# Adding pairs of exponential tiles by accumulating DMAs in the softmax sums of a fused attention and mixture-of-experts block

## The chip, the cores and the metric

The kernel runs on one core of one Trainium2 chip, in one launch. The metric is the device time of a run in microseconds. Of the kernel before there are three runs, and one more that was profiled.

## The reference, cut to what matters

The reference is a transformer block with layer norms behind both halves: attention with LoRA on its four projections, then a mixture of eight experts plus a shared expert. The change lies in the attention, and there in the sums of the softmax.

```python
q, k, v = (split(lora_linear(x, ...)) for each)      # x: 2 x 1024 x 512, 16 heads of 32
scores = jnp.einsum('bhqd,bhkd->bhqk', q, k) * HEAD_DIM ** -0.5
attn = jax.nn.softmax(scores, axis=-1)               # divides by the sum over the 1024 keys
out = jnp.einsum('bhqk,bhkd->bhqd', attn, v)
x = layernorm(x + lora_linear(out, Wo, ...))
x = layernorm(x + moe(x))
```

## The kernel before

The program has three parts: projections with the folding of LoRA, attention, and the output projection's end with the experts. In the profile the attention runs from 158 to 624 us of the span.

The attention is cut into **16 units**, u = 0 to 15. A unit is one group of four heads and 512 queries of one batch. It has **eight steps**, kc = 0 to 7, one for each block of 128 keys; step t is 8u + kc, and "k3" means the step in which kc is 3. The order inside a step is written out by hand and holds on every engine (`manual_schedule` over all five), so an instruction waits for all that stand before it on its own engine. In a step stand:

- four scores matmuls (`st`, L569, one for each head), each followed on ScalarE by the exponential (L578). Two heads share one tile of 128x1024, so a step fills two tiles `pts[t, 0]` and `pts[t, 1]`, called pair 0 and pair 1 here. The tiles lie in `PTB = 13` buffers of one pool.
- four matmuls of another kind (`s`, L182), which compute the scores of the unit to come with queries in the rows, twelve steps ahead (`LEAD`). VectorE takes a maximum out of each (L190). They go through three PSUM banks: a fourth `s` matmul waits until the first has been read. The maxima of a unit are transposed in k4 (`finish_max`, L200) and shift the exponentials of a later unit.
- between the second and the third scores matmul, `av_step` of the step before: eight matmuls (L599) that multiply the exponentials of step t - 1 with the values.

The sums over the keys are formed by whole-tile additions. `add_step(t, pr)` (L588) makes the tile of kc = 0 the accumulator `accs[u, pr]` at no cost and adds the tiles of kc = 1 to 6 to it; kc = 7 is not added but goes into the sum matmuls directly (`DIRECT`). An addition is on VectorE where `ON_DVE` says so, for (1, 0) and (2, 1), and otherwise on GpSimd: ten on GpSimd and two on VectorE in each of the units 0 to 13. The addition (1, 0) is issued early, within k1 (`EARLY`); the others are issued in `av_step`, one step after their tile's. The last two units have a table of their own (`DVE_END`).

In k3 of the next unit, `finish` (L622) multiplies the two accumulators and the two tiles of kc = 7 with ones: 16 matmuls behind that step's `av` matmuls. ScalarE copies the sums out, small DMAs on the SP queue carry them through DRAM to a reciprocal on VectorE (`invert`, issued at the end of k4) and back, and in k7 the outputs are scaled (`normalize`).

GpSimd has other work in the same queue: it adds the output bias to a residual tile (`add_res`, L674) in k1 of each unit from 1 on, and in k5 of the units 12 and 13 as well. During the units 8 and 9 the output projection of the first batch is woven in (L691), which makes these two units about 10 us longer.

Of the kernel before, what the change touches and what calls it, by code (L numbers as in the profile page):

```python
# [2 lines left out]

# [10 lines left out]
ALU = mybir.AluOpType  # L14
# [39 lines left out]
FIN = 3  # L54
REC = 4
XTB = 5
ON_DVE = ((1, 0), (2, 1))
EARLY = (1, 0)
OPROJ_AT = (65, 67, 69, 71, 73, 75, 77, 79)
RES_AT = tuple(8 * i + 6 for i in range(8)) + (70, 78, 86, 94, 98, 102, 106, 110)  # L60
# [9 lines left out]
DVE_END = {  # L70
    NU - 2: ((1, 0), (2, 1), (4, 1), (5, 1), (6, 0), (6, 1), (7, 0), (7, 1)),
    NU - 1: ((1, 0), (2, 0), (3, 0), (4, 0), (5, 0), (6, 0), (6, 1)),
}
# [19 lines left out]
def kernel(  # L93
# [3 lines left out]
    pe, act, dve, pool, sp = nc.tensor, nc.scalar, nc.vector, nc.gpsimd, nc.sync  # L97
# [74 lines left out]
    mts, pts, avs, accs, vts = {}, {}, {}, {}, {}  # L172
# [377 lines left out]
    with ph2, tc.manual_schedule(engines={mybir.EngineType.PE}):  # L550
# [31 lines left out]
        def add_step(t, pr):  # L582
            u, kc = t // 8, t % 8
            if kc == 0:
                accs[u, pr] = pts[t, pr]
            elif kc not in direct(u):
                eng = dve if (kc, pr) in DVE_END.get(u, ON_DVE) else pool
                eng.tensor_tensor(accs[u, pr], accs[u, pr], pts[t, pr], ALU.add)  # L588

        def early(t, pr):  # L590
            return t // 8 not in DVE_END and (t % 8, pr) == EARLY

        def av_step(t):
            u, kc = t // 8, t % 8
            g = u // 2
            if kc == 0:
                avs[u] = avp.tile([P, 512], F32, name=f"av{u}", tag="av")
            for h in range(4):
                pe.matmul(  # L599
                    avs[u][32 * h : 32 * h + 32, :],  # L600
                    vts[g][:, kc, 32 * h : 32 * h + 32],
                    pts[t, h // 2][:, h % 2, :],
                    start=kc == 0,
                    stop=kc == 7,
                    skip_group_check=True,
                )
            for pr in range(2):
                if not early(t, pr):
                    add_step(t, pr)

        def direct(u):
            return () if u in NO_DIR else DIRECT
# [98 lines left out]
        for t in range(NS):  # L711
            u, k = t // 8, t % 8
# [17 lines left out]
            if t:  # L730
                between[1].append(lambda: av_step(t - 1))
                if u and k == (FINE if u == NU - 1 else FIN):
                    between[1].append(lambda: finish(u - 1))
# [19 lines left out]
            if t - NS >= OPROJ1:  # L753
                next(op10, None)
        av_step(NS - 1)
        finish(NU - 1)
        normalize(NU - 1, (0,))
# [302 lines left out]
    for st in range(NB):  # L1060
# [18 lines left out]
        if st == NB - 3:  # L1079
            reads_xd(  # L1080
                sp.dma_start(
                    out=meta, in_=xd_d[:, D : D + 2].rearrange("(j p) c -> p j c", p=P)
# [7 lines left out]
    with tc.manual_schedule(engines=MAN4):  # L1090
        last = None
        for e in range(E):
            nxt = e + 1
            hss = []
            for c in range(6):
# [32 lines left out]
                if e:  # L1128
                    for hf in range(2):
                        j = 2 * (e - 1) + hf  # L1130
# [7 lines left out]
        for hf in range(2):  # L1138
            j = 2 * (E - 1) + hf
# [65 lines left out]
```

## Time and profile before

| what | value |
|---|---|
| median of three runs | 1076.01 us (1075.66 to 1076.06) |
| time of the profiled execution | 1076.59 us |
| its span in the profile | 1074.9 us, so 1.69 us lie around the span |
| granted TensorE clock | 0.993 |
| busy share of the span, PE / VectorE / ScalarE / GpSimd | 97 / 70 / 49 / 53 % |
| attention, 158.15 to 624.36 us: busy PE / VectorE / ScalarE / GpSimd | 451.0 / 416.6 / 290.4 / 385.1 us of 466.2 |

The span is the time from the first to the last instruction of one profiled execution. Busy time is a union of the intervals in which an engine works, so a share near one says that an engine is hardly ever without an instruction, and not that it is at its peak.

### The profile page before, as it was taken

How to read it: one execution, taken by the hardware profiler on the slowest of the kernel's cores; microseconds unless marked ns; L12 is line 12 of the kernel's file. 1: busy time of each engine (PE TensorE's matmuls, PEld its weight loads, DVE VectorE, ACT ScalarE, POOL GpSimd, SP SyncE). 2: the span in 40 equal slices, each digit the busy share in tenths (PEclk: the TensorE clock that was granted, in tenths of full speed). 3: DMA queues.
4: the chain of work that ended last, by engine and by line, in shares of the span. 5: the costliest groups of instructions: out<-in, count | busy, mean ns of one | idle time of the engine just before them, and what ended most of it. 6: DMA issues, size and time to landing. Idle time of an engine off the chain costs nothing. (4 is left out here: it accounts for less than half of the span.)

```text
span 1074.9 us, 16446 instructions
## 1 busy us (share of the span) xinstructions
PE 1038.9 (97%) x5992; PEld 742.9 (69%) x5992; DVE 748.3 (70%) x1217; ACT 530.1 (49%) x1026; POOL 573.1 (53%) x379
## 2 busy tenths in 40 slices
PE   8999999999999999999999999999999999999996
PEld 6888774444444455544444369889999998888885
DVE  6732788999999987799998784233522556777762
ACT  5422215666666655556666756222222455555552
POOL 5000007888888877868899575000050045666674
PEclk8999999999999999999999999999999999999999
DMA  8866860141414242042520123000082556777731
GB/s 279 288 219 202 252 195 25 52 110 48 103 47 106 71 109 70 22 90 70 119 81 22 51 60 109 20 21 20 31 240 95 161 184 207 234 234 235 237 107 59
DMA packets 77585, 131.24 MB, mean 122 GB/s; under 512 B 14344, under 2 KB 23048, under 8 KB 77504
## 3 DMA queue, kind: packets, MB, share of 16 engines
q1 hardware_dynamic: 73664, 117.59, 37.6%
q0 software_dynamic: 3840, 12.60, 3.3%
q8 instruction: 47, 0.77, 0.3%
q14 instruction: 34, 0.28, 0.1%
HBM read 96.10 MB, written 33.80 MB: 121 GB/s over the span
## 5 line engine op out<-in xcount | busy, mean ns | idle before, releaser
L588 POOL TENSOR_TENSOR pt<-pt,pt 128x1024 f32<-128x1024 f32 x151 | 360.5, 2413 | 207.7 <-ACT pt L578 190.6
L190 DVE TENSOR_REDUCE mt<-s 128x1 f32<-128x512 f32 x512 | 323.4, 680 | 39.7 <-PE s L182 39.6
L578 ACT ACTIVATE pt<-st 128x512 f32<-128x512 f32 x512 | 270.8, 602 | 141.4 <-PE st L569 137.6
L569 PE MATMUL st<-qs,ks 98*128 98x512 f32 x512 | 215.6, 432 | 1.9 <-ACT pt L578 1.2
L182 PE MATMUL s<-ks,qs 96*128 96x512 f32 x512 | 203.0, 404 | 12.7 <-DVE mt L190 11.5
L569 PEld LDWEIGHTS st<-qs,ks 98*128 98x128 f32 x512 | 96.0, 189 | 136.4 <-issue 87.2
L817 POOL TENSOR_TENSOR w2s<-w2r,w2s 128x512 fp32r<-128x512 f32 x42 | 65.7, 1582 | 127.0 <-ACT w2s L816 103.1
L829 PE MATMUL h<-xthe,w13s 128*128 128x256 f32 x704 | 131.4, 284 | 1.5 <-DVE hs L850 1.5
L182 PEld LDWEIGHTS s<-ks,qs 96*128 96x128 f32 x512 | 97.2, 190 | 41.3 <-DVE mt L190 26.8
L829 PEld LDWEIGHTS h<-xthe,w13s 128*128 128x128 f32 x704 | 111.0, 191 | 3.0 <-DVE hs L850 2.7
L829 PE MATMUL h<-xtle,w13s 128*128 128x256 f32 x352 | 100.2, 285 | 0.0
L588 DVE TENSOR_TENSOR pt<-pt,pt 128x1024 f32<-128x1024 f32 x43 | 91.4, 2131 | 3.3 <-ACT pt L578 2.9
L599 PE MATMUL av<-pt,vt 128*32 128x512 f32 x512 | 75.0, 605 | 0.0
L599 PE MATMUL av<-pt,x1b 128*32 128x512 f32 x512 | 68.8, 609 | 0.0
L829 PEld LDWEIGHTS h<-xtle,w13s 128*128 128x128 f32 x352 | 67.3, 191 | 0.7
L977 POOL DMA_INDIRECT xd_d<-x1a,slot_i x8 | 8.0, 996 | 111.8 <-DVE slot_i L974 109.7
L873 PE MATMUL y<-w2s,hs 128*128 128x512 f32 x260 | 62.7, 394 | 2.9 <-POOL w2s L817 2.9
L873 PEld LDWEIGHTS y<-w2s,hs 128*128 128x128 f32 x260 | 47.4, 188 | 15.7 <-POOL w2s L817 6.7
L297 PE MATMUL o<-xh,wh 128*128 128x512 f32 x128 | 51.1, 399 | 3.0 <-ACT wh L271 3.0
L312 ACT ACTIVATE oh<-o,bqk_sb 128x512 fp32r<-128x512 f32 x32 | 22.0, 690 | 59.0 <-PE o L297 56.5
L297 PE MATMUL o<-xl,wh 128*128 128x512 f32 x128 | 50.9, 398 | 0.0
L297 PE MATMUL o<-xh,wl 128*128 128x512 f32 x128 | 50.9, 397 | 0.0
(819 smaller groups left out, 1758.5 us busy)
## 6 DMA issues: line engine op xcount, KB each, us to landing
qs<-qkd SPq DMA_DIRECT2D x48, 256.0 KB, 5.6
ks<-qkd SPq DMA_DIRECT2D x24, 512.0 KB, 6.8
x1a<-in_w_dram SPq DMA_DIRECT2D x24, 512.0 KB, 6.8
w2r<-in_w_dram SPq DMA_DIRECT2D x42, 256.0 KB, 3.2
qkd<-oh SPq DMA_DIRECT2D x32, 256.0 KB, 2.7
qkd<-ol SPq DMA_DIRECT2D x32, 256.0 KB, 2.6
x1b<-in_w_dram SPq DMA_DIRECT2D x16, 512.0 KB, 5.7
x1b<-in_wT_dram SPq DMA_DIRECT2D x16, 256.0 KB, 5.3
```

What stands on the lines that cost most here:

```text
L182: pe.matmul(s1, Qs[u % 3][0:96, h, qt * P : qt * P + P], Ks[g % 2][0:96, h, kh * 512 : kh * 512 + 512], start=True, stop=True,)
L190: dve.tensor_reduce(mts[u][:, c, kh : kh + 1], s1, AX.X, ALU.max)
L297: pe.matmul(o, lhs, rhs, start=k + i == 0, stop=k + i == KC + 1)
L312: act.activation(oh, o, AF.Identity, bias=bias)
L569: pe.matmul(sb, Ks[g % 2][:, h, kc * P : kc * P + P], Qs[u % 3][:, h, :], start=True, stop=True,)
L578: act.activation(pts[t, h // 2][:, h % 2, :], sb, AF.Exp, scale=SCALE)
L588: eng.tensor_tensor(accs[u, pr], accs[u, pr], pts[t, pr], ALU.add)
L599: pe.matmul(avs[u][32 * h : 32 * h + 32, :], vts[g][:, kc, 32 * h : 32 * h + 32], pts[t, h // 2][:, h % 2, :], start=kc == 0, stop=kc == 7 ...
L817: pool.tensor_tensor(hl[:, 1, :], raw, f(hl[:, 0, :]), ALU.subtract)
L829: pe.matmul(hp[:, j * 256 : j * 256 + 256], lhs, rhs[:, k, :], start=n == 0, stop=n == 11,)
L873: pe.matmul(o, lhs, rhs, start=n == 0, stop=n == 16)
L977: sc_ = pool.indirect_dma_start(out=xd_d, out_offset=bass.IndirectOffsetOnAxis(ap=slot_i[:, i : i + 1], axis=0), in_=x1[i // 8][:, i % 8, ...
```

## The change

In the units 0 to 13 the tiles of kc = 2 are no longer added to the accumulators by an engine. In their place GpSimd's queue issues, in `av_step` of kc = 3, one DMA for each pair that adds the tile of kc = 2 to the tile of kc = 3 in SBUF (`accum_op=ALU.add`, 512 KB each). The sum of both, standing in the tile of kc = 3, is added to the accumulator on GpSimd one step later, behind the additions of kc = 4. VectorE keeps the addition (1, 0) alone. The units 14 and 15 are as before.

```diff
-ON_DVE = ((1, 0), (2, 1))
+ON_DVE = ((1, 0),)
+DMA_LATE = 1
...
-            for pr in range(2):
-                if not early(t, pr):
-                    add_step(t, pr)
+
+            for d, pr in product((0, DMA_LATE), range(2)):
+                j = kc - d
+                if u in DVE_END:
+                    if d == 0:
+                        add_step(t, pr)
+                elif j == 3 and d == 0:
+                    pool.dma_start(out=pts[t, pr], in_=pts[t - 1, pr], accum_op=ALU.add)
+                elif (j == 3) == (d > 0) and j >= 0 and j != 2 and not early(t - d, pr):
+                    add_step(t - d, pr)
```

The order of a unit's work on GpSimd becomes: the addition (1, 1); the two DMAs; the additions (4, 0), (4, 1), (3, 0), (3, 1), (5, 0), (5, 1), (6, 0), (6, 1). In the built program GpSimd goes from 377 to 391 instructions and VectorE from 1212 to 1198.

## The prediction

> **What bounds the kernel now.** I read the page's busy rows and groups first, then the timelines of VectorE, PE and GpSimd in unit 5 (299.35 to 327.19 us), then the DMA rows. The page:
>
> ```profile
> L588 POOL TENSOR_TENSOR pt<-pt,pt 128x1024 f32<-128x1024 f32 x151 | 360.5, 2413 | 207.7 <-ACT pt L578 190.6
> L190 DVE TENSOR_REDUCE mt<-s 128x1 f32<-128x512 f32 x512 | 323.4, 680 | 39.7 <-PE s L182 39.6
> L182 PE MATMUL s<-ks,qs 96*128 96x512 f32 x512 | 203.0, 404 | 12.7 <-DVE mt L190 11.5
> ...
> L588 DVE TENSOR_TENSOR pt<-pt,pt 128x1024 f32<-128x1024 f32 x43 | 91.4, 2131 | 3.3 <-ACT pt L578 2.9
> ...
> L977 POOL DMA_INDIRECT xd_d<-x1a,slot_i x8 | 8.0, 996 | 111.8 <-DVE slot_i L974 109.7
> ```
>
> PE is the engine that is never without work. It loses only 11.5 us to VectorE by this row, but delays that hide inside stretched matmuls add to that, so I take step lengths. In PE's timeline the scores matmuls that open the steps of unit 5 stand at 299.35, 302.42, 305.49, 308.95, 313.73, 317.71, 321.05, 324.13 and 327.19: steps k0 to k7 of 3.07, 3.07, 3.46, 4.78, 3.98, 3.34, 3.08 and 3.06 us, in all 27.84. An undisturbed step is 3.07; k3 has the sums in addition. What can be won is in k2 (0.4 over) and k4 (0.9 over). PE, timeline, unit 5:
>
> ```profile
> 306.49 0.49 PE L182 MATMUL s<-ks,qs 96*128 96x512 f32 x1
> ...
> 310.86 1.90 PE L622 MATMUL sm<-pt,ones 128*32 128x512 f32 x16
> ...
> 315.09 0.50 PE L182 MATMUL s<-ks,qs 96*128 96x512 f32 x1 [0.50 <-DVE mt L190]
> 315.53 1.07 PE L599 MATMUL av<-pt,x1b 128*32 128x512 f32 x8
> ```
>
> VectorE and GpSimd over the same stretch (start, duration, count at the end, idle time before in brackets):
>
> ```profile
> 304.61 1.23 DVE L588 TENSOR_TENSOR pt<-pt,pt 128x1024 f32<-128x1024 f32 x1
> 305.75 2.48 DVE L190 TENSOR_REDUCE mt<-s 128x1 f32<-128x512 f32 x4
> ...
> 311.08 3.35 DVE L588 TENSOR_TENSOR pt<-pt,pt 128x1024 f32<-128x1024 f32 x1
> 314.36 1.28 DVE L190 TENSOR_REDUCE mt<-s 128x1 f32<-128x512 f32 x2
> ```
>
> ```profile
> 303.19 1.28 POOL L674 TENSOR_TENSOR x1a<-x1a,bo_bc 128x512 f32<-128x512 f32 x1
> 306.20 7.16 POOL L588 TENSOR_TENSOR pt<-pt,pt 128x1024 f32<-128x1024 f32 x3 [1.73 <-ACT pt L578]
> 314.58 14.09 POOL L588 TENSOR_TENSOR pt<-pt,pt 128x1024 f32<-128x1024 f32 x6 [1.23 <-DVE pt L588]
> ```
>
> The reader is to see this: the same VectorE addition takes **1.23 us** at 304.61, while GpSimd is idle (304.47 to 306.20), and **3.35** at 311.08, where a GpSimd addition is under way until 313.36 (306.20 + 7.16). 3.35 is 2.28 of waiting and 1.07 of adding. The long one keeps VectorE from the maxima, so the `s` matmul due at 314.43 starts at 315.09.
>
> **What the Trainium skill says.** "SBUF — State Buffer", section "Who interferes with whom": a VectorE instruction with two SBUF inputs contends with a GpSimd instruction that reads SBUF, and the second one to issue blocks until the first is done; `tensor_reduce` never contends on trn2. The trace agrees: 1.23 against 3.35, and maxima every 0.62 us beside a busy GpSimd. "DMA: Bandwidth & Descriptors", section "SWDGE vs HWDGE vs iDMA": a DMA that accumulates is issued from GpSimd, whose cores write its descriptors. The trace of before has only indirect ones (0.96 to 1.05 us of GpSimd each, mostly). "Collectives: The Full Stack", section "The bandwidth ceiling: the fold count and why AG ≠ RS ≠ AR": an adding transfer reads two sources for each write, and ran at half of a copy's rate. No row of before shows an accumulating DMA.
>
> **The change part by part.** Clock zero is the start of k4.
>
> *VectorE's addition (2, 1) goes* (14 of them). Without it `s` starts at 314.43, `av` 0.32 later at 314.75 and not at 315.53: **0.77 us** of k4 in each of the units 1 to 7, 10, 11 and 12, 7.7 in all. Unit 13 has a k4 of 3.70, worth 0.5. In unit 0 no sums cover the addition and PE shows 2.18 us idle at 174.54: 2.4. In units 8 and 9 the projection's matmuls lie between, idle 0.53 and 0.56: 0.6 each. Sum **-11.8**.
>
> *GpSimd's chain moves.* One addition per unit goes (10 to 9, 14 in all, 2.35 us each back to back), but the unit's eight late additions now stand behind two DMAs that wait for the `av` matmuls of kc = 3, which PE ends 2.09 after k4 starts. Before, the additions began in k2, at 306.20, as tiles came. Issue: 0.15 idle ahead of a DMA in the trace, 0.97 each, 0.305 between two, 0.03 to the next addition: the first addition starts at 2.09 + 0.15 + 0.97 + 0.305 + 0.97 + 0.03 = **4.5**. Additions then end at 6.9, 9.2, 11.6, 13.9, 16.3, **18.6**, 21.0 and 23.3.
>
> *What this meets.* VectorE's remaining addition comes 2.19 after k1 starts (304.61 - 302.42), which is 3.21 + 3.34 + 3.08 + 3.06 + 3.07 + 2.19 = **17.95**. Before, GpSimd was idle then. Now its sixth addition runs until 18.6, so VectorE is blocked for 0.65 first. Its 1.23 cost k2 0.4 (three PSUM banks absorb the rest), and all beyond costs PE in full: **+0.65** in k1 or k2 of the units 1 to 8, 11 and 12, 6.5 in all. Units 9 and 10 follow the long units, where GpSimd is done by then: 0. Unit 13 follows a unit with a bias addition in k5 (1.25): 1.9 against 0.75 lost there now, +1.15. In unit 14 the sums of 13 come about 1.2 late for the same 1.25. Sum **+8.85**.
>
> *The sums.* With VectorE's addition between them the last two GpSimd additions end at 24.4; `sm` is due at 22.93 + 1.91 = 24.84. Slack 0.45, hidden, and gone with half a microsecond more.
>
> *The transfers.* They share 16 DMA engines with SP's: nothing large is in flight (loads come in k0 and k6), but the small ones that carry the reciprocal are (`r` lands 3.05 after k4 starts, `rb` at 9.9 for a use at 12). The first must land by 9.2, 7.0 after its issue; the second by 11.6, 8.1 after. Loads of 512 KB land in 3.9 to 6.8 us, 256 KB in 2.7 to 5.6. Twice the reading makes 512 KB like 1 MB: from the quiet values 2.7 and 3.9, about 6.3, an estimate. So it is in time, and costs nothing; if the 6.8 were doubled, 13.6, GpSimd would be 6.6 late in each unit.
>
> *Buffers.* In the built program the exponential tiles of the next unit reuse freed tiles; the closest is (5, 0), 3 us after GpSimd's (1, 1) addition ends. No SP instruction moves; ScalarE has the same work.
>
> *Sum:* -11.8 + 8.85 = **-3.0 us** on the profiled 1076.59, which is 0.58 above the median: 1076.01 - 3.0 = **1073.0**.
>
> *Bounds of the unknown issue time* i (nearest row 0.97). Lateness is 2(i - 0.97) and weighs on ten units. At 0.7 the block is 0.11: -8.4. Under 0.64 the sixth addition is over and VectorE meets the whole seventh, 2.35: +14. At 1.12 the gain is gone. At 1.9 (two descriptors read per written one, twice the row) the lateness is 1.86: about +16.
>
> **The rivals.** *(a) The remaining addition is blocked longer (slower).* Place: VectorE in k1, against a GpSimd chain that is later, or earlier, by a fraction of 2.35 us. For it: 18.6 and 17.95 are 0.65 apart, and reading both operands may make the issue dearer than an indirect one. Against: the nearest row is steady. It decides from an issue of 1.12 us; at 1.5 the loss is 10 x 1.06 - 3.0 = +7.6, **1083.6**. *(b) The transfers land late (slower too).* GpSimd waits in front of (3, 0), `sm` waits for GpSimd, and every microsecond late costs one in 11 units: 1 us late makes -3 + 11 = +8, **1084**; 2 us, 1095. For it: a margin near 1 us over my estimate. Against: loads of the same size land within 6.8. *(c) The GpSimd chain falls just behind VectorE's addition,* issue about 0.7: **1067.6**. *(d) No difference:* what k4 gains k1 loses, **1076**, at issues near 1.1.
>
> **How the numbers follow.** The forecast with (c) as its good end, 1065 to 1073.8: 0.5. (d): 0.12. (a): 0.2. (b): 0.18. A measurement of this kernel tells 0.2%, 2.15 us, from no change. Faster 0.5, same 0.12, slower 0.38. The range is 1065 to 1091: down to no block at all with a little more, up to (a) at 1.9 or (b) at 1.6 us late. The forecast's own range is 1065 to 1074.
>
> **What would show it.** Right: k4 near 3.2 us, no VectorE L588 in k3, DMA issues near 1 us, a VectorE addition in k1 of about 1.9 us, k2 near 4.1, `sm` not waiting. Wrong: a VectorE addition of 3 us in k1 with k2 over 4.9 (a); GpSimd idle in front of L589 with a DMA as the releaser, and k3 over 5 (b); a k4 that stays at 3.9, which would mean that (2, 1) was not what delayed it.

## The result, and the profile after

The changed kernel takes **1180.59 us**, the median of four runs (1179.74 to 1183.92), against 1076.03 for the kernel before, run beside it: a ratio of **1.0978**, with a 95% interval from 1.0955 to 1.1001. The profiled execution took 1179.74 us with a span of 1178.0 and a granted TensorE clock of 0.946, where before it was 0.993.

First the groups of the page that answer to those of before. Behind the bar stand busy time, the mean of one in ns, and the idle time in front with what ended most of it.

```profile
L589 POOL TENSOR_TENSOR pt<-pt,pt 128x1024 f32<-128x1024 f32 x137 | 340.7, 2881 | 167.5 <-PE s L183 147.7
L191 DVE TENSOR_REDUCE mt<-s 128x1 f32<-128x512 f32 x512 | 324.4, 680 | 105.2 <-PE s L183 104.9
...
L183 PE MATMUL s<-ks,qs 96*128 96x512 f32 x512 | 215.4, 428 | 72.8 <-DVE mt L191 72.7
...
L615 POOL DMA_DIRECT2D pt<-pt x28 | 25.1, 1041 | 149.0 <-PE st L570 142.8
L589 DVE TENSOR_TENSOR pt<-pt,pt 128x1024 f32<-128x1024 f32 x29 | 91.4, 3161 | 6.0 <-PE av L600 2.8
```

The reader is to see three things. VectorE makes 29 additions instead of 43 and spends the same 91.4 us on them, so one takes 3.16 us instead of 2.13. The maxima `mt` and the `s` matmuls now wait for each other: 105 us on VectorE's side, 73 on PE's, where PE lost 11.5 before. And an addition on GpSimd reads 2.88 us, although additions in a row still begin 2.33 apart.

The step lengths say where. Unit 5 began at 299.35 before and begins at 334.02 now; in us:

| | k0 | k1 | k2 | k3 | k4 | k5 | k6 | k7 | unit |
|---|---|---|---|---|---|---|---|---|---|
| before | 3.07 | 3.06 | 3.46 | 4.78 | 3.97 | 3.34 | 3.08 | 3.06 | 27.83 |
| after | **6.79** | 3.08 | **10.28** | 4.80 | 3.21 | 3.34 | 3.07 | 3.07 | 37.64 |

k4 lost 0.76 us, as the change was to do. k0 grew by 3.7 and k2 by 6.8. PE's timeline of this unit (start, duration, idle time before and what ended it):

```profile
336.04 0.49 PE L183 MATMUL s<-ks,qs 96*128 96x512 f32 x1 [1.62 <-DVE mt L191]
...
341.84 1.07 PE L600 MATMUL av<-pt,x1b 128*32 128x512 f32 x8
...
349.70 0.79 PE L183 MATMUL s<-ks,qs 96*128 96x512 f32 x1 [4.96 <-DVE mt L191]
350.43 1.94 PE L600 MATMUL av<-pt,x1b 128*32 128x512 f32 x8
```

Both stalls end with a maximum of VectorE's. What VectorE did meanwhile:

```profile
334.70 0.70 DVE L669 TENSOR_TENSOR av<-av,rb 128x512 f32<-128x512 f32 x1 [2.13 <-DMA rb<-rd]
...
343.04 6.01 DVE L589 TENSOR_TENSOR pt<-pt,pt 128x1024 f32<-128x1024 f32 x1
348.97 2.47 DVE L191 TENSOR_REDUCE mt<-s 128x1 f32<-128x512 f32 x4
```

GpSimd over the same stretch:

```profile
323.99 1.77 POOL L615 DMA_DIRECT2D pt<-pt  x2 [13.73 <-PE st L570]
325.14 19.30 POOL L589 TENSOR_TENSOR pt<-pt,pt 128x1024 f32<-128x1024 f32 x8
343.82 1.85 POOL L682 TENSOR_TENSOR x1a<-x1a,bo_bc 128x512 f32<-128x512 f32 x1
345.06 2.90 POOL L589 TENSOR_TENSOR pt<-pt,pt 128x1024 f32<-128x1024 f32 x1
```

**The stall in k2** is the addition (1, 0) at 343.04. The eighth addition of GpSimd's row ends at 325.14 + 19.30 = 344.44, the residual's at 345.67, (1, 1) at 347.96, and VectorE's addition ends 1.09 later. It was held out not for the addition under way but until GpSimd's whole row was over. It depends on none of these three by its data.

**The stall in k0** is `normalize`, which waits for `rb`. The list of transfers has the median time from issue to landing at the end of a row; after:

```profile
pt<-pt POOLq DMA_DIRECT2D x28, 512.0 KB, 6.0
...
rd<-r SPq DMA_DIRECT2D x14, 8.0 KB, 5.1
```

before:

```profile
rd<-r SPq DMA_DIRECT2D x14, 8.0 KB, 1.6
```

The 8 KB of `rd` land 5.1 us after their issue instead of 1.6. In unit 1, counted from the start of k4, the two accumulating transfers are issued at 2.64 and 3.22 and land at 7.15 and 9.71; `rd` is issued at 4.89, and the first `rb` follows at 9.94, 0.2 us after the second transfer is in. `rb` lands at 12.8, and VectorE's scaling, which stands in k7 and was due at 12 before, slips into k0.

**A third part** no instruction waits for. After a stall PE's matmuls are slow: the `av` block at 350.43 takes 1.94 us, that at 341.84 took 1.07. Windows of unit 5 (the clock is the column behind the five engines):

```profile
337.13:340.54 3.41, 3.41 (x12) 1.37 (x12) 1.98 (x5) 1.36 (x3) 3.41 (x3) 0.50 0.48 115
...
343.89:349.60 5.71, 0.86 (x4) 0.38 (x2) 5.71 (x3) 1.61 (x4) 4.06 (x3) 0.80 0.00 0
349.60:354.17 4.57, 4.47 (x14) 1.98 (x14) 2.46 (x5) 0.79 (x2) 0.00 (x0) 0.50 0.00 0
354.17:358.97 4.80, 4.80 (x33) 2.14 (x32) 2.23 (x5) 2.39 (x5) 0.00 (x0) 1.00 0.00 0
```

Behind the idle 5 us the granted clock is 0.50 until k3 begins. Of the 7.2 us that k2 has over an undisturbed 3.07, about 5.1 are the gap in front of the `s` matmul and 2.1 are slow matmuls. The Trainium skill, "TensorE: Matmul & The Clock Gate", section "Part 1: The HAM clock gate (the "warmup" mystery)", says that after an idle window of some 3.4 us the clock is gated to 4/8 and comes back after a busy window. The two values are those of this trace, 0.50 and 1.00. The idle time is not: in k0 PE stood still for only 1.62 us, until 336.04, and the clock was 0.50 from 337.13 to 340.54 all the same.

### The profile page after: what moved, and what is told of

Its sections match the earlier page's. It is cut to its first block, busy times and chain, and to the rows that moved or that the text cites. A ratio compares the mean times of both kernels' runs of the same rounds, so it can differ in the third digit from the quotient of the medians.

```text
span 1178.0 us, 16463 instructions
## 1 busy us (share of the span) xinstructions
PE 1080.2 (92%) x5992; PEld 757.1 (64%) x5992; DVE 753.0 (64%) x1203; ACT 533.1 (45%) x1026; POOL 562.9 (48%) x393
## 4 chain that ended last, share of the span: by engine, by line
PE 62%; DVE 14%; DMA 10%; issue 5%; POOL 4%; ACT 2%; SPq 1%; POOLq 0%; DVEq 0%; ACTq 0%
PE av L600 9%; PE st L570 8%; PE o L298 7%; PE s L183 7%; DVE pt L589 5%; DMA rd<-r 5%; DVE mt L191 4%; PE op L699 3%; PE v L324 3%; PE h L837 3%; POOL w2s L825 3%; PE sm L630 2%; DMA rb<-rd 2%; DVE w13s L518 2%; SPq L658 1%
## 5 line engine op out<-in xcount | busy, mean ns | idle before, releaser
L589 POOL TENSOR_TENSOR pt<-pt,pt 128x1024 f32<-128x1024 f32 x137 | 340.7, 2881 | 167.5 <-PE s L183 147.7
L579 ACT ACTIVATE pt<-st 128x512 f32<-128x512 f32 x512 | 274.2, 602 | 209.4 <-PE st L570 203.1
L183 PE MATMUL s<-ks,qs 96*128 96x512 f32 x512 | 215.4, 428 | 72.8 <-DVE mt L191 72.7
L570 PE MATMUL st<-qs,ks 98*128 98x512 f32 x512 | 228.6, 457 | 2.1 <-ACT pt L579 1.2
L570 PEld LDWEIGHTS st<-qs,ks 98*128 98x128 f32 x512 | 102.9, 203 | 157.5 <-issue 103.6
L183 PEld LDWEIGHTS s<-ks,qs 96*128 96x128 f32 x512 | 105.4, 206 | 101.9 <-DVE mt L191 86.3
L615 POOL DMA_DIRECT2D pt<-pt x28 | 25.1, 1041 | 149.0 <-PE st L570 142.8
L589 DVE TENSOR_TENSOR pt<-pt,pt 128x1024 f32<-128x1024 f32 x29 | 91.4, 3161 | 6.0 <-PE av L600 2.8
L600 PE MATMUL av<-pt,vt 128*32 128x512 f32 x512 | 81.6, 661 | 0.0
L600 PE MATMUL av<-pt,x1b 128*32 128x512 f32 x512 | 80.3, 704 | 0.0
L881 PEld LDWEIGHTS y<-w2s,hs 128*128 128x128 f32 x260 | 47.4, 188 | 15.8 <-POOL w2s L825 6.7
```

The source lines that it names most:

```text
L183: pe.matmul(s1, Qs[u % 3][0:96, h, qt * P : qt * P + P], Ks[g % 2][0:96, h, kh * 512 : kh * 512 + 512], start=True, stop=True,)
L570: pe.matmul(sb, Ks[g % 2][:, h, kc * P : kc * P + P], Qs[u % 3][:, h, :], start=True, stop=True,)
L579: act.activation(pts[t, h // 2][:, h % 2, :], sb, AF.Exp, scale=SCALE)
L600: pe.matmul(avs[u][32 * h : 32 * h + 32, :], vts[g][:, kc, 32 * h : 32 * h + 32], pts[t, h // 2][:, h % 2, :], start=kc == 0, stop=kc == 7 ...
L881: pe.matmul(o, lhs, rhs, start=n == 0, stop=n == 16)
```

## The experiments

A single run is compared with the kernel before on the same chip, where that took 1087.9 us (E1 to E4), 1075.5 (E5 to E8), 1087.7 (E14 to E16) or the median named.

### E1 and E2: the transfers left out, or turned into plain copies

```diff
-   pool.dma_start(out=pts[t, pr], in_=pts[t - 1, pr], accum_op=ALU.add)
+   pass                                                          # E1
+   pool.dma_start(out=pts[t, pr], in_=pts[t - 1, pr])            # E2
```

> The changed kernel without its 28 accumulating DMAs; the tiles of kc = 2 are left out of the sums of units 0 to 13, and 1.0 is added to each sum in the copy on ScalarE so that none is zero. Two theories on the 6.6 us that k2 grew by: (train) VectorE's addition in k1 waits until GpSimd's whole unbroken row of additions is over, not just the one under way; (DMA) the DMAs bring it about. Train: the row now starts when the exponentials of k4 are there, and holds its nine tile additions and the bias addition without a gap until about 24 us after k4 starts; VectorE's addition comes at 18, takes 4 to 7 us, k2 is 6 to 9.5 us. DMA: k2 is back at 3.5. On the 3.7 us that k0 grew by: (queue) the reciprocal's store waits behind the accumulating DMAs; then k0 is back at 3.1. (late chain) GpSimd's later additions delay it; then k0 stays near 6.8. Train with queue: 1076 - 12 + 11 x 5 = about 1120 (1095 to 1140); DMA with queue: 1065 to 1072.

> The changed kernel with its 28 DMAs as plain copies of the same tiles from the same queue: the tile of kc = 2 replaces that of kc = 3 in place of being added (kc = 3 is left out of the sums), and 1.0 is added to each sum. Queue theory, by volume: the reciprocal's store still lands with the second copy; copies read half, so the second lands about 5.0 us after k4 starts plus 3, near 8.2 and not 9.7, and k0 grows by 1.5 to 2.5 us instead of 3.7. If the accumulation itself holds the engines: k0 is 3.1, at most 3.5. k2 stays near 10 by the train theory, since GpSimd's row is as long. About 1160 by volume, 1140 by accumulation.

E1 leaves the tiles of kc = 2 out of the sums and E2 those of kc = 3; so that no sum is zero, both add 1.0 to each in ScalarE's copy, as E16 does below. E1 took 1185.57 us, 1.090 of the kernel before; E2 1201.97, 1.105. In E1 the first `rb` is issued 6.2 to 6.6 us after k4 begins in most units, and k0 is back to 3.07. That shows the cause of k0. E2 lies between: `rb` at 7.6 to 9.4, k0 mostly 3.1 to 4.3. But E1 was hardly faster than the change. VectorE in its unit 5:

```profile
332.46 1.87 DVE L191 TENSOR_REDUCE mt<-s 128x1 f32<-128x512 f32 x3
334.35 7.23 DVE L589 TENSOR_TENSOR pt<-pt,pt 128x1024 f32<-128x1024 f32 x1
```

and GpSimd:

```profile
318.20 18.77 POOL L589 TENSOR_TENSOR pt<-pt,pt 128x1024 f32<-128x1024 f32 x8 [15.40 <-ACT pt L579]
336.94 1.25 POOL L682 TENSOR_TENSOR x1a<-x1a,bo_bc 128x512 f32<-128x512 f32 x1
338.17 2.33 POOL L589 TENSOR_TENSOR pt<-pt,pt 128x1024 f32<-128x1024 f32 x1
```

VectorE comes earlier in the row and waits that much longer, 7.2 us with its own addition, again to the end of (1, 1) at 340.50. So the wait in k2 needs no transfer. Counted from k4, the row ends 2.5 us sooner than in the changed kernel (24.1 instead of 26.6), but k3 takes 7.31 us instead of 4.80 and uses that up, for the clock stays low longer:

```profile
338.39:352.04 13.65, 9.81 (x37) 3.87 (x41) 8.35 (x9) 2.39 (x4) 2.10 (x1) 0.50 0.00 0
```

That is 13.65 us at 0.50 in one unit, where unit 5 of the changed kernel has 10.24. So taking k0's delay away alone gains nothing. In both kernels the clock changes at distances that are multiples of 3.41 us, and a unit of 37.6 us is eleven of these; that this fixes the unit's length is not shown.

### E3: the addition (1, 0) on GpSimd

```diff
-ON_DVE = ((1, 0),)
-EARLY = (1, 0)
+ON_DVE = ()
+EARLY = None
```

> The changed kernel with the addition (1, 0) on GpSimd too (ten tile additions there, none on VectorE in units 0 to 13), so that nothing of VectorE's meets GpSimd's row. Train: k2 is 3.1 us in all units, while k0 keeps its 6.8 (queue); a unit is 27.1 + 3.7 = 30.8 us, the whole about 1076 - 16 + 12 x 3.7 = 1104 (1095 to 1115). If something else than that addition stretches k2 (tiles that come free late, the DMAs): k2 stays over 5 and the whole over 1130. GpSimd's row of ten ends 2.4 us later, near 25 after k4 starts, which the longer k0 covers.

1123.40 us, 1.033. The times of E1 to E3 are all above what was expected, on a chip where the kernel before too took 1.1% longer than beside the changed one. With no addition of VectorE's in the units 0 to 13, k2 is 3.06 in all units to 7 and k4 3.27; k0 keeps its 5.2 to 9.1. This shows the cause of k2, and now k0's delay counts: units 2 to 6 take 28.8 to 31.2 us.

### E7, E5 and E6: the transfers issued one step later

```diff
 # av_step of kc = 4, behind the additions (4, 0) and (4, 1)
+   pool.dma_start(out=pts[t - 1, pr], in_=pts[t - 2, pr], accum_op=ALU.add)
 # av_step of kc = 6, behind (6, 0) and (6, 1)
+   add_step(t - 3, pr)
 # E5: and (1, 0) on GpSimd, as in E3.  E6: and VectorE's (1, 0) at the end of k3
```

> The changed kernel with its two accumulating transfers issued one step later, behind the additions (4,0) and (4,1), and the additions (3,0) and (3,1) behind (6,0) and (6,1). VectorE keeps (1,0) at its place. Theory: the softmax sums' reciprocals are then stored before the 1 MB is on its way, so `rb` is issued about 7 us after k4 begins and k0 is back to 3.1 us (6.85 in the changed kernel), while GpSimd's row is as unbroken as before, VectorE's addition still waits 4 us or more in it and k2 stays at 9 to 12 us: 1.06 to 1.10 of the kernel before. Rival (the reciprocal is late because VectorE is, not because of the transfers): k0 stays above 6 us. Rival (VectorE's wait comes from the transfers' issue ahead of the row): k2 falls below 5 us and the time below 1.01.

> As the one with the later transfers, and the addition (1,0) on GpSimd, so that VectorE has no addition left in the units that the change touches. Theory (the two waits and the slow matmuls behind them were all that the change lost): k0 3.1, k2 3.1, k4 3.2 us, a unit of 26.7 to 27.1 us instead of 27.8, 0.985 to 0.992 of the kernel before. Rival (GpSimd is full: ten additions of 2.36 us, the residual's 1.25 and two issues of 1 us are 26.9 us of a unit, and it holds the exponential tiles too long): the exponentials wait for tiles, units of 28.5 us or more, 1.01 to 1.05.

> As the one with the later transfers, and VectorE's addition (1,0) moved from step k1 to the end of step k3, where GpSimd's row of the unit before is over. Theory (VectorE's addition is cheap where GpSimd has no row under way): the addition takes 1.2 to 2.4 us, k0 and k2 3.1 us, k3 or k4 up by at most 1.2 us, a unit of 26.9 to 27.8 us, 0.985 to 1.00 of the kernel before. Rival (GpSimd's row has moved back with the transfers, and its addition (1,1) or the next row meets VectorE there too): the addition takes 3.5 us or more, k4 above 5 us, 1.02 to 1.06.

E7: 1180.18 us, 1.097. `rb` is first issued at 6.2 to 7.7 and k0 is 3.7 to 3.9 in six units, and the time is what it was: E1's finding once more, with the transfers present (k3 is about 4.8 and 6.8 in turn). E5: 1079.67, 1.004. k2 3.07 and k4 3.27 as expected, but k0 is 3.6 to 5.0, and 9.0 in unit 7, because the transfers now go out at 6.4 together with the four `rb`, of which some land only at 11.3 to 11.6. Unit 14 takes 33.8 us instead of 26.9 as well, for VectorE's addition takes 6.20 us there. E6: 1095.13, 1.018. VectorE's addition takes 1.22 us in all units, so it is cheap where GpSimd has no row under way; both named outcomes missed, for the loss is in k0, 4.5 to 6.4 in most units. Its trace shows the wait of E5, only longer: the transfers go out 0.6 us behind the first `rb`, and VectorE's scaling in unit 5 waits 1.69 us for `rb`:

```profile
299.86 0.70 DVE L670 TENSOR_TENSOR av<-av,rb 128x512 f32<-128x512 f32 x1 [1.69 <-DMA rb<-rd]
```

### E4, E8: the wait by itself

Kernels of another kind: GpSimd adds 128x1024 tiles in a row, on one accumulator or on two in turn, and VectorE makes one addition of its own behind some reductions.

```python
for k in range(n):
    pool.tensor_tensor(acc[k % turns], acc[k % turns], src, ALU.add)
for r in range(nred):
    dve.tensor_reduce(red, rows[:, 0:2, :], AX.XY, ALU.max)
dve.tensor_tensor(dva, dva, src, ALU.add)
```

> The block by itself, nothing of the block's computation: seven cases, in each of which GpSimd does n additions of 128x1024 while VectorE takes one maximum over 1024 elements and then adds two SBUF tiles of 128x1024. n = 1, 2, 4, 8 with two accumulators in turn (as in the kernel), then 2, 4, 8 on one accumulator, where each GpSimd addition waits for the one before. Train: with two accumulators VectorE's addition takes about 1.2 us plus all that is left of the row: near 2, 4.5, 9 and 18 us. Lock for one instruction: 2 to 3.5 us whatever n is. On one accumulator I expect VectorE to get in at the first gap, 2 to 3.5 us for every n, as in the last units of the profile before.

> Measures the disputed wait by itself, not the reference: in each case GpSimd makes eight additions of 128x1024 and VectorE one of its own behind one to eight reductions of 1.1 us, so that it comes in the first, second, third or fourth addition of GpSimd's row. Twelve cases: two accumulators in turn with 1, 3, 5, 8 reductions; one accumulator with 3 and 5; two accumulators with a source tile of its own for each addition (5); with a PSUM reduction just ahead of VectorE's addition (5); and with sources that ScalarE writes one after the other while the row runs (two accumulators 1 and 5, one accumulator 5, two accumulators 3). Theory A (VectorE gets in only at a gap in GpSimd's row, and additions that take turns on two accumulators leave none once the row runs): alone 1.2 us; with two accumulators and 3, 5, 8 reductions it waits to the end of the row, 12 to 17 us; with one accumulator at most 3.6 us. Theory B (the wait is for one instruction of GpSimd's at most, whatever comes behind it): 1.3 to 3.6 us in every case, and the kernel's long waits have another cause. Theory C (only rows whose additions have their own fresh sources hold VectorE out): long waits in the cases with own or fed sources alone.

My theory of a row that never lets go fell here. In E4 VectorE's addition took 2.39 us in rows of 2, 4 and 8, on one accumulator or two: the rest of the addition under way, and then its own 1.07, while GpSimd's next addition stretched from 2.34 to 3.2 or 3.3 us. In E8 all twelve cases took 1.2 to 3.4 us. That is the rule of the prediction, and the kernel breaks it.

### E9: what the kernel has and these rows lacked

```diff
+   for q in range(2):
+       pool.dma_start(out=big[1][:, q], in_=big[0][:, q], accum_op=ALU.add)
    for k in range(8): ...
```

> Measures the wait by itself again, not the reference, with what the kernel has and the rows measured so far lacked: GpSimd makes eight additions on two accumulators, VectorE one. Twelve cases: plain (3 reductions of VectorE's ahead of its addition); two accumulating 512 KB transfers issued by GpSimd ahead of its row (3 reductions; 5; 5 with one accumulator); two plain transfers ahead of it (5); one addition of half the width in the row; VectorE idle and waiting for ScalarE's tile; the same with an accumulator that GpSimd, then GpSimd and TensorE have touched; that with PSUM reductions and fed sources; all tiles at other addresses; a row of 14 with VectorE coming in the seventh. Theory A (what an accumulating transfer's issue does to GpSimd's row, 2.97 us for an addition at a distance of 2.33, keeps VectorE out): the three cases with accumulating transfers wait for two additions or more, over 4.5 us, the others 1.2 to 3.6. Theory B (VectorE gets in only if it does not come from a semaphore wait with its queue empty): the cases that wait for ScalarE take over 4.5 us, the others 1.2 to 3.6. Theory C (a long row): only the last case does. If no case exceeds 3.6 us, what keeps VectorE out in the kernel isn't among these.

Theory A, and more than it. With two transfers issued by GpSimd in front of a row on two accumulators VectorE's addition took 18.1 and 15.8 us, which is the rest of the row. With plain transfers, which I had put among the short ones, it took 15.2. With the accumulating transfers and **one** accumulator, whose additions have a gap of 0.08 us in front, it took 2.19. The other eight cases took 1.2 to 2.5; in three of them (the plain one, the tiles at other addresses and the row of 14) VectorE's addition missed the row it was meant for. E12 has the plain row again and E14 the row of 14.

### E12: the issue or the traffic

> Measures the wait by itself once more, not the reference: eight additions of GpSimd's on two accumulators, one of VectorE's. Twelve cases: plain; two 512 KB transfers issued by SyncE instead of GpSimd; one transfer of 16 columns issued by GpSimd; GpSimd's two accumulating transfers, with two additions in series on each accumulator at the head of the row; the same transfers, with the row begun only 4 us later, when ScalarE's tile is ready; a transfer issued behind the third addition, VectorE coming in the second; a one-column power of GpSimd's ahead of the row; a memset of two partitions ahead of it; a row begun after a rest without a transfer; TensorE and ScalarE at work beside the row; those with a rest and SyncE's transfers; GpSimd's two transfers once more. Theory A (it is the issue on GpSimd, whatever its size): the cases of GpSimd's transfers wait for the rest of the row, over 10 us, but for the one with additions in series at its head, 3.6 us at most; SyncE's transfers cost 1.2 to 3.6. Theory B (it is the traffic of 1 MB): SyncE's case waits as long and the one of 16 columns doesn't. Theory C (other work of GpSimd's[...] does it too, as in the kernel without transfers): the power or the two-partition memset waits for the row; or the rest ahead of the row or the other engines' work does. If of these four none exceeds 3.6 us, what kept VectorE out in the kernel without transfers stays open.

| in front of the row of eight on two accumulators | VectorE's addition, us |
|---|---|
| nothing | 1.63 |
| two 512 KB transfers issued by SyncE | 2.50 |
| one transfer of 16 columns issued by GpSimd | **14.84** |
| GpSimd's two transfers | **15.82** |
| the same, two additions in series on each accumulator first | 1.21 |
| the same, the row begun only after a rest | 1.74 |
| a memset of two partitions | **13.48** |
| a one-column power | 3.16 |

The remaining cases took 1.7 to 2.5. VectorE in the case with 16 columns, after four reductions of one form:

```profile
59.79 4.58 DVE L106 TENSOR_REDUCE red<-rows 128x1 f32<-128x1024 f32 x4
64.29 14.84 DVE L107 TENSOR_TENSOR dva<-dva,src 128x1024 f32<-128x1024 f32 x1
```

GpSimd there:

```profile
58.87 0.73 POOL L84 DMA_DIRECT2D big<-big  x1
59.62 18.43 POOL L101 TENSOR_TENSOR acc<-acc,src 128x1024 f32<-128x1024 f32 x8
```

59.62 + 18.43 = 78.05, and VectorE ends at 79.13. So it is the issue on GpSimd, whatever its size, and not the traffic. With a rest in front of the row, or with additions in series under way when VectorE comes, the wait is short, and work of GpSimd's on few partitions brings the long one about too, without a transfer. What in GpSimd does it is not shown. Long records are not its mark: behind the accumulating transfers an addition reads 2.9 to 3.0 us at a distance of 2.30, but 2.3 to 2.4 behind the 16 columns, the memset and the plain transfers of E9, and in E1 and E2, where VectorE was kept out as well.

### E14: candidates for the kernel without transfers

> The wait by itself, not the reference, for what could keep VectorE out in a row ahead of which GpSimd issues nothing: GpSimd's row on two accumulators, one addition of VectorE's. Eleven cases: plain; the second addition late because ScalarE's tile is; the third late; most additions on tiles that ScalarE makes one by one; VectorE at PSUM reductions during the whole row; that with TensorE at work and one addition of half the width; a row of 14 with VectorE coming in its sixth; the two-partition memset with additions in series at the row's head; the memset and then a rest; a 16-column transfer and two short copies of GpSimd's in series ahead of the row; an affine select ahead of it. Theory A ([...]the kernel without transfers has its cause elsewhere): 1.2 to 3.6 us in all cases, but for the affine select, which is open. Theory B (a row that waits inside for ScalarE does it): one of the cases with late tiles waits over 4.5 us. Theory C (VectorE's PSUM reductions beside the row): those cases wait over 4.5 us.

All eleven cases took 1.25 to 3.06 us: rows that wait inside for ScalarE, VectorE at PSUM reductions, a row of 14, an affine select, the memset with a pair in series or a rest behind it, and a transfer of 16 columns with two short copies in series behind it. That is theory A, and with it E1's cause is still open; its row too begins behind a rest, of 15.4 us.

### E11, E15 and E16: the order of GpSimd's row in the kernel

```diff
 # order of GpSimd's row
-(4,0) (4,1) (3,0) (3,1) (5,0) (5,1) (6,0) (6,1)
+(4,0) (3,0) (4,1) (3,1) (5,0) (6,0) (5,1) (6,1)      # E11
+(4,0) (3,0) (4,1) (3,1) (5,0) (5,1) (6,0) (6,1)      # E15; E16: the same without transfers
```

> The changed kernel with the additions of GpSimd's row in another order: (4,0), (3,0), (4,1), (3,1), (5,0), (6,0), (5,1), (6,1), so that every second one continues on the accumulator of the one before and leaves a gap of about 0.08 us in front of it, where additions that take turns on the two accumulators follow one another without one. VectorE keeps (1,0) at its place. Theory (a gap is what VectorE needs to get in): its addition waits for at most two of GpSimd's, 1.2 to 4.5 us instead of 5.7 to 10, k2 falls to 4 to 7 us from 10, 1120 to 1150 us. Rival (gaps are of no account): 5.7 us or more, k2 9 to 13 us, 1175 us or more.

> The changed kernel with the order of four additions of GpSimd's row changed alone: (4,0), (3,0), (4,1), (3,1) at its head, the rest as it was. Theory (a pair of additions in series on one accumulator ends the state that the transfers' issue leaves GpSimd in, as in isolation): VectorE's addition waits for one addition of GpSimd's at most, 1.2 to 3.6 us, k2 4 to 7 us, 1130 to 1145 us as with every second addition in series. Rival (the gap has to lie just where VectorE waits): 5.7 us or more, k2 9 to 10 us, 1175 us or more.

> The same order without the two transfers, so that the third tiles (2,0) and (2,1) are missing from the sums, and 1.0 is added to each sum. Theory (the pair in series at the row's head is enough here too, whatever put GpSimd into that state without a transfer): the addition takes 1.2 to 3.6 us instead of 7.0 to 8.2, k0 3.1, k2 4 to 6 us, a unit of 28 to 31 us, 1080 to 1110 us. Rival (the state without a transfer is another one, which a pair doesn't end): 7 us or more, 1175 us or more.

E11: 1138.51 us, 1.057 of 1076.98. VectorE's addition takes 1.2 to 3.4 us in the units 1 to 13 and k2 is 3.4 to 7.2, in the same kernel with the same instructions. Unit 3, VectorE (the residual's addition has the line L684 here):

```profile
257.07 3.31 DVE L589 TENSOR_TENSOR pt<-pt,pt 128x1024 f32<-128x1024 f32 x1
```

GpSimd:

```profile
254.44 4.86 POOL L589 TENSOR_TENSOR pt<-pt,pt 128x1024 f32<-128x1024 f32 x2
259.24 2.25 POOL L684 TENSOR_TENSOR x1a<-x1a,bo_bc 128x512 f32<-128x512 f32 x1
```

VectorE gets in as soon as (6, 1) is over, at 259.30, and it is GpSimd's residual addition that stretches, from about 1.2 us to 2.25. So the order of the row is what keeps VectorE out, not its amount of work. E15, with the pairs at the head alone, took 1189.22 us, 1.093: the addition still takes 6.3 to 6.5 us in the units 2, 4, 6, 8, 11 and 12 and 11.2 in unit 1, and the short ones between them come only after a k0 or k1 so long that the row is nearly done. E16, 1185.46 or 1.090, is E1 over again, at 7.2 us and more. These are the rivals' figures, and E15's rival says that the gap has to lie just where VectorE waits. In isolation it did: VectorE came during the third addition in E12 and the second in E14, while those in series were under way, so these cases do not show that a pair lets VectorE in later in the row.

### E10, E13 and E17: a version that beats both

```diff
 # E10: E5 with the two transfers behind (5, 0)
-   (4,0) (4,1) DMA DMA (5,0) (5,1) (6,0) (6,1) (3,0) (3,1)
+   (4,0) (4,1) (5,0) DMA DMA (5,1) (6,0) (6,1) (3,0) (3,1)
 # E13: and in unit 14 (1, 0) on GpSimd, (3, 0) on VectorE
 # E17: E10 with the residual rows of the second half earlier
-RES_AT = ... + (70, 78, 86, 94, 98, 102, 106, 110)
+RES_AT = ... + (66, 68, 70, 72, 74, 76, 80, 88)
```

> As the kernel with later transfers and (1,0) on GpSimd, with the two transfers issued one addition later again, behind (5,0), some 10.5 us after k4 begins, when `rb` has landed. Theory (what was left of k0's excess, 3.6 to 5.0 us instead of 3.07 and 9 in unit 7, is `rb` sharing the queues with the transfers): k0 3.1 in all units up to 7 and from 11, a unit of 26.7 to 27.0 us against 27.84, 1062 to 1068 us, 0.987 to 0.993 of the kernel before. Rival (GpSimd's 26.9 us of work in a unit is the bound by then, and the tiles that the late transfers hold come free too late): the exponentials wait at k0, k1 or k3, a unit of 27.4 us or more, 1073 us or more.

> The kernel with the transfers behind (5,0) and (1,0) on GpSimd, and in unit 14, whose additions the change doesn't touch, VectorE's addition (1,0) given to GpSimd and (3,0) to VectorE instead. Theory (what is left to lose there is VectorE waiting 7.5 us in step k2 of unit 14 for the row of unit 13): the unit takes 27 to 30 us instead of 34.5, 1067 to 1071 us, 0.991 to 0.996 of the kernel before. Rival (GpSimd is that late by then that the sums of unit 13 wait for it at k3, whoever adds (1,0)): 33 us or more, 1074 us or more.

> The kernel with the transfers behind (5,0) and (1,0) on GpSimd, with the residual rows of the second half loaded, and their additions of 1.1 to 1.3 us made by GpSimd, in units 8 to 11 instead of 8 to 14. Theory (what it still loses is GpSimd's row falling behind in units 12 to 14, where two residual additions a unit come on top of a row that fills the unit: k4 of unit 12 is 6.9 us, and VectorE waits 7.5 us in k2 of unit 14): unit 12 at 26.7 to 27.7 us instead of 30.4, unit 14 at 27 to 30 instead of 34.5, units 8 to 10 as they were, 1063 to 1069 us, 0.987 to 0.993 of the kernel before. Rival (units 9 to 11 take over the lag, or unit 14's wait has nothing to do with the residual): 1073 us or more.

E10: 1075.07 us against 1076.98, ratio 0.9977 (0.9967 to 0.9988). The mechanism came as expected, k0 at 3.05 to 3.17 and units of 26.7 us, but two things eat most of it: every second unit loses 0.8 to 1.2 us in k4, and GpSimd falls behind in units 12 to 14 (k4 of unit 12 is 6.93; in unit 14 VectorE's addition waits 7.46 us, k3 13.9). E13: 0.9984 (0.9972 to 0.9995); unit 14 takes 34.46 us, as in E10, because VectorE's next addition, (2, 1), now stands still for 5.77 us until GpSimd's late row has got to (1, 1), and then waits beside its (2, 0):

```profile
579.82 3.35 DVE L589 TENSOR_TENSOR pt<-pt,pt 128x1024 f32<-128x1024 f32 x1 [5.77 <-POOL pt L589]
```

So the rival was right that GpSimd is that late whoever adds (1, 0), though not about the place: k3, where it put the wait, is 4.79, and k4 is 11.72. E17: **1077.93 against 1087.1, ratio 0.9916** (0.9892 to 0.9939). Unit 12 falls from 30.4 to 27.75 and unit 14 from 34.5 to 31.7, not to 30. PE's row of E17, for the idle time in front of `s`:

```profile
L183 PE MATMUL s<-ks,qs 96*128 96x512 f32 x512 | 200.5, 399 | 6.9 <-DVE mt L191 4.2
```

6.9 us against 72.8 in the changed kernel. Its attention runs from 157.85 to 613.98, 456.1 us where the kernel before needs 466.2 in its trace, on another chip.

## Why the prediction was wrong, point by point

- **VectorE's addition (2, 1) goes, 0.77 us of k4.** Right: k4 is 3.21, down from 3.97. Unit 0 gained 3.7 where 2.4 was put.
- **The chain's start.** The issues measure 0.87 and 1.18 us, 1.03 in the mean, near the 0.97 taken; but the second begins 0.58 after the first and the first addition 1.15 after it. The chain starts at 3.79 instead of 4.5. This term was mis-sized, and by the prediction's own rule not harmlessly: it is an issue time of 0.61 in its sum, under the 0.64 at which the sixth addition is over and VectorE meets the seventh, +14. So even the rule of one addition made the change slower with the issue that came.
- **"VectorE is blocked for 0.65 first."** This is the step that failed. The prediction carried over from one wait in the profile of before, 3.35 us against 1.23, that VectorE waits for the addition under way. In that profile the addition was the last of a row in units 1 to 7, so that wait could not tell one addition from a row. VectorE did get into the middle of a row in unit 14 of before, in 2.12 us, but there GpSimd's second addition ends at 595.10 and the third begins at 595.18, on the same accumulator, with the gap of a row in series:

```profile
594.06 2.12 DVE L588 TENSOR_TENSOR pt<-pt,pt 128x1024 f32<-128x1024 f32 x1 [1.32 <-ACT pt L578]
590.41 4.69 POOL L588 TENSOR_TENSOR pt<-pt,pt 128x1024 f32<-128x1024 f32 x2
595.18 3.23 POOL L588 TENSOR_TENSOR pt<-pt,pt 128x1024 f32<-128x1024 f32 x1
```

Measured in the changed kernel: 4.6 to 5.0 us of waiting in the units 2 to 6, 8 and 12, 5.9 in unit 13, 9.0 in unit 1, not 0.65; by E3 and E11 that wait is the loss in k2. The Trainium skill's page that the prediction used, "SBUF — State Buffer", section "Who interferes with whom", has the second to issue blocked until the first is done; E4 and E8 agree (1.2 to 3.4 us), E9 and E12 do not (13 to 18 us, for up to eight instructions of GpSimd's), and the measurement decides.

- **"So it is in time, and costs nothing."** Half right. In most units the transfers land about 4.5 and 6.5 us after their issue, before the 7.0 and 8.1 that were needed. In the units 0, 6 and 9 the second lands only 7.7 to 8.2 us after, and GpSimd's (3, 1) begins 0.2 to 0.8 us late. But the prediction named `r` and `rb` as small transfers in the same stretch and then costed them at nothing; `rd`, which lies between them, landed at 9.89 in unit 3, 0.2 us behind the second transfer, where it had landed at 6.93. The Trainium skill, "DMA: Bandwidth & Descriptors", section "Issuing engines are not separate DMA queues", says that transfers of all issuers run on the same 16 engines and interleave; here 8 KB on SP's queue were through only when GpSimd's 1 MB was. By E1 and E7 taking it away alone gains next to nothing in the changed kernel; by E3, where VectorE's wait is gone, k0 is 5.2 to 7.5 us in units 2 to 6, 2.1 to 4.5 over 3.07.
- **PE's clock was not in the sum.** A wait of 5 us was priced at 5 us, and cost 7.2 in k2; in k0, of 3.7 us, about 1.9 are slow matmuls.
- **The sums' slack** held: k3 is 4.80.
- **The rivals.** (a) had the right place, VectorE in k1 and k2, and the right sign, but took the same rule of one addition, and by it 2.35 was the most that could be lost. (b) hardly happened: GpSimd waited for a transfer in three units, for less than 1 us, and k3 stayed under 5 in the units 1 to 7.

Sum over the units: 0 gains 3.7, 9 and 10 gain 1.1 together, 14 loses 6.1 behind unit 13's late row; 2 to 6 and 12 lose 9.6 to 9.8 each, the units 1, 7, 8, 11 and 13 another 42 together. That is about 102 of the 103.1 us between the two spans.

**What stays open:** which condition makes GpSimd's row keep VectorE out in the kernel without transfers (E1, E16), since no case of E14 brought it about, what in GpSimd makes it do so behind a transfer or a memset, and what delays k4 in every second unit of E10.

## What to carry to other kernels

Before an addition of VectorE's is left beside a row of GpSimd's, ask how long the whole row is and not how long one of its instructions is; put it where GpSimd rests, or give GpSimd's row an order in which instructions in series leave a gap just there. When a bulk transfer is added, list the small ones on which a later step waits, issue it behind them, and look at each landing afterwards. Price a PE stall of several microseconds higher than its length, for the clock behind it is low.

## What the runs showed that I had not expected

- A transfer of 16 columns issued by GpSimd in front of a row made VectorE wait 14.8 us; 1 MB issued by SyncE left it at 2.5. A memset of two partitions did the same, 13.5.
- With one accumulator the additions of a row begin 0.08 us after the end of the one before, and that gap was enough: 2.19 us instead of 15.8.
- An accumulating transfer of 512 KB within SBUF takes GpSimd 0.87 us to issue for the first and 1.18 for the second of a pair, against 0.57 and 0.53 for a plain copy (E2), and lands 4.5 and 6.5 us after its issue.
- Two delays in one unit did not add: taking away k0's 3.7 us alone changed the ratio by less than 0.01 in E1 and E7. VectorE still waited to the end of GpSimd's row, and the row's earlier end (2.5 us in E1) went into slow matmuls.
- The clock fell to 0.50 behind a wait of PE's of 1.62 us, and not only behind those of 5.
